# Group norms on ScalarE, and the last image's closing stages in row blocks beside the last scan

## The chip, the cores and the metric

The kernel runs on one core of one Trainium2 chip. The metric is the device time of one execution in microseconds (us), from the first to the last instruction on the core and what lies around it. Before the change the median of three runs is 14916.63 us (14892.47 to 14927.26). Profiles are single executions recorded by the hardware profiler; all times inside the kernel come from such a record.

## The reference

Four images of 96 channels and 64 x 64 points pass through four layers. Every layer is `x = x + layer(gn(x))`, where `gn` is a group norm with 32 groups of 3 channels:

```python
def _gn(v, G=32, eps=1e-5):
    g = v.reshape(B_, G, C_ // G, H_, W_)
    m = jnp.mean(g, axis=(2, 3, 4), keepdims=True)
    s = jnp.var(g, axis=(2, 3, 4), keepdims=True)
    return ((g - m) / jnp.sqrt(s + eps)).reshape(v.shape)
```

Layer 0 is an attention over a sampled image with a neighbourhood step. Layer 1 projects to 192 channels, convolves, and runs a state-space scan of 16 states in four directions (rows forward, rows backward, columns forward, columns backward); the four results are summed, layer-normed, gated and passed through a convolution block. Layer 2 is a 3 x 3 sharpening convolution. Layer 3 has a second such scan, `h = h * exp(d * A) + (d * u) * b`, `y = sum over states of h * c`, again in four directions, followed by what the kernel calls `finish`:

```python
y = oy[:, 0] + inv[:, 0] + why + invwhy            # four directions
y = layernorm(y) * silu(z) @ ow.T                   # norm, gate, output projection
y = x1 + x2 * g                                     # skip branch
y = layernorm over channels
up = conv1x1(y[:48]); low = conv1x1(y[48:])         # squeeze to 24 each
Y1 = conv3x3(up, groups=2) + conv1x1(up); Y2 = concat(conv1x1(low), low)
out = softmax(mean over points of concat(Y1, Y2)) * concat(Y1, Y2)
out = (first half + second half) @ fin_w.T + fin_b
```

Only the mean over all points couples distant rows in this last part; the 3 x 3 convolution couples neighbouring rows; everything else is per point.

## The kernel before

**Scans.** There are eight scans, one per image and scan layer, in the order `SCANS`. A scan has four directions ("ways"), each of 4 chunks of 1024 points and two halves of the channels: 32 groups. A group has 12 units; a unit is 8 channels x 16 states on 128 partitions and 1024 points. So a scan has 384 units, and the kernel 3072. The function `unit` writes one unit's instructions: SyncE fetches `rep` (the step sizes, broadcast) four units ahead (`fetch`, L1827); ScalarE turns it into the decay two units ahead (`decays`, L1835); TensorE spreads the input into PSUM two units ahead (`drive`); VectorE multiplies that by `b` one unit ahead (`times_b`, L1849) and runs the scan (`scan`, L1856); POOL multiplies by `c` (`times_c`, L1868); every third unit TensorE sums the states (`collect`). At the end of a group `output` puts the result into `yo`, and SyncE stores it to `y_row` or `y_col` at the start of the next unit (L1904). The next groups' step sizes and inputs are made by `prepare`, in steps between the units.

**Work beside a scan.** All other layers of the images are Python generators: `first` (layer 0 and the start of layer 1), `second` (the end of layer 1, layer 2, the start of layer 3) and `third` (the end of layer 3). `BESIDE` says which runs beside which scan: scans 0, 3, 4 have a first, scans 1, 2, 5, 6 a second, the last scan the thirds of images 0, 1 and 2. A generator yields a number when it has issued a step; `unit` resumes it up to twice, once ahead of `decays` and once ahead of `times_b`, within a budget: `PACE` (3.5) a unit, less 2.1 in every third unit. What is left of a stage at unit 365 of a scan is written out at once (`work.run()`). The first stage of image 0 runs alone before the scans (to 702 us), the third of image 3 alone after them. Inside the scans the order on each engine is that of the program; each engine works its own instructions in that order.

**Group norm** (L1039): eight `bn_stats` of 512 points and an aggregate on VectorE, two small matmuls that average over the three channels of a group, a root on ScalarE, and four `tensor_scalar` on VectorE that write the result. Each first and each second has two.

**The end of layer 3** (`third`, `finish`). `directions` loads `y_col` and `y_row` and adds them on POOL (L1391). `layer_norm` runs over 8 chunks of 512 points: mean by matmul, subtraction on VectorE (L1153), square on ScalarE (L1155), sum of squares by matmul; then one root (L1165) and one reciprocal (L1167) for all chunks; then per chunk the product and `gate` (L1575, L1576). The output projection adds `skip3` (L1590). A second norm is followed per chunk by `squeeze`; then the convolution, the mean and softmax, and per chunk the final product (L1687), which reads `res2` through tile `o` and stores the result.

Of the kernel before, what the change touches and what calls it, by code (L numbers as in the profile page):

```python
# [9 lines left out]
F32 = mybir.dt.float32  # L10
# [28 lines left out]
          (("first", 3),), (("second", 2),), (("second", 3),), (("third", 0), ("third", 1), ("third", 2)))  # L39
# [854 lines left out]
def streams(ctx: ExitStack, tc: tile.TileContext, x, wts, cst, out, wat, cat, flag):  # L894
# [144 lines left out]
    def group_norm(src, dst):  # L1039

        st = small.tile([96, 8, 6], F32, name="gn_st")
# [23 lines left out]
        for j in range(4):  # L1065
            nc.vector.tensor_scalar(dst[:, 16 * j : 16 * j + 16, :], img(src)[:, 16 * j : 16 * j + 16, :],
                                    g[:, 0:1], g[:, 1:2], ALU.subtract, ALU.mult)
            yield 1
# [67 lines left out]
    def layer_norm(pool, V, n, gains, each):  # L1136

        acc = held()
        sq = {}

        def add(j):
            for h in range(n):
                mm(acc[:8], cv("means")[:96, n - 1, 7 - j : 15 - j], sq.pop((j, h)),
                   j == 0 and h == 0, j == 7 and h == n - 1)

        for j in range(8):
# [5 lines left out]
            for h in range(n):  # L1152
                nc.vector.tensor_sub(V[:, h, js], V[:, h, js], p1[:96])  # L1153
                t = pool.tile([96, PCH], F32, name="ln_sq", bufs=2 * n)
                nc.scalar.activation(t, V[:, h, js], AF.Square)  # L1155
                sq[j, h] = t
            yield n
            if j:
                add(j - 1)
                yield  # L1160
                yield n
        add(7)
        yield
        r = pool.tile([8, PCH], F32, name="ln_r", bufs=1)
        nc.scalar.activation(r, acc[:8], AF.Sqrt, bias=eps[:8])  # L1165
        yield n
        nc.vector.reciprocal(r, r)  # L1167
        yield 3
        for j in range(8):
            js = bass.ts(j, PCH)  # L1170
            p = bank()
            mm(p[:96], ident[:8, j : j + 1].to_broadcast([8, 96]), r)
# [383 lines left out]

    def third(b):

        with tc.tile_pool(name="p3x", bufs=1) as PX:
            V = yield from directions(PX, b)  # L1560
            yield from finish(PX, b, V)

    def finish(PX, b, V):
        with tc.tile_pool(name="p3", bufs=2) as pool:
            w = staged(pool, "l3_in", "l3_out")

            def gate(j):
                js = bass.ts(j, PCH)
                xz = pool.tile([96, PCH], F32, name="xz", bufs=2)
                nc.sync.dma_start(out=xz, in_=gate3[b][:, js])  # L1570
                for h in range(2):
                    p = bank()
                    mm(p[:96], w["l3_in"][:, E + 96 * h : E + 96 * h + 96], xz)
                    yield
                    nc.scalar.activation(p[:96], p[:96], AF.Silu)  # L1575
                    nc.vector.scalar_tensor_tensor(out=V[:, h, js], in0=V[:, h, js],  # L1576
                                                   scalar=wv("l3_ss_outn_b")[:, h : h + 1], in1=p[:96],
                                                   op0=ALU.add, op1=ALU.mult)
                    yield 1

            yield from layer_norm(pool, V, 2, wv("l3_ss_outn_g"), gate)
            for j in range(8):
                js = bass.ts(j, PCH)
                x2 = pool.tile([96, PCH], F32, tag="tmp", name="x2")
                nc.sync.dma_start(out=x2, in_=skip3[b][:, js])
                p = bank()
                for h in range(2):
                    mm(p[:96], w["l3_out"][:, h, :], V[:, h, js], h == 0, h == 1)
                yield
                nc.vector.scalar_tensor_tensor(out=V[:, 0, js], in0=x2, scalar=0.5, in1=p[:96],  # L1590
                                               op0=ALU.mult, op1=ALU.add)
                yield 2
        with tc.tile_pool(name="p4", bufs=2) as pool:

            up = pool.tile([96, PADW, W], F32, name="up", bufs=1)
            for s in (up[:, 0, :], up[:, PADW - 1, :], up[0:32, :, 0:1], up[64:96, :, W - 1 : W]):
                nc.gpsimd.memset(s, 0.0)
            sq3 = pool.tile([96, 3, 32], F32, name="sq3", bufs=1)
            nc.gpsimd.memset(sq3, 0.0)
            gw = pool.tile([96, 3, C], F32, name="gw", bufs=1)  # L1600
            nc.gpsimd.memset(gw, 0.0)
            pw = pool.tile([96, C], F32, name="pw", bufs=1)
# [8 lines left out]
            low = pool.tile([24, L], F32, name="low", bufs=1)  # L1611

            def squeeze(j):
# [13 lines left out]
                mm(q[:24], wv("l3_sq")[:, 1, :], v)  # L1627
                yield
                nc.scalar.copy(low[:, js], q[:24])
                yield 1  # L1630

            yield from layer_norm(pool, V[:, 0:1, :], 1, wv("l3_ln_g"), squeeze)
            w = staged(pool, "l3_y2", "l3_fin")

            sums = pool.tile([96, 2, 8], F32, name="csums", bufs=1)
            for j in range(8):
                js = bass.ts(j, PCH)
                p = bank()
                for t in range(3):
                    mm(p[:96], gw[:, t, :], up[:, 8 * j + t : 8 * j + t + 8, :], t == 0, t == 2)  # L1640
                    if t < 2:
                        yield (1,)
                yield
# [440 lines left out]
```

## Time and profile before

| | us |
|---|---|
| median of 3 runs | 14916.63 |
| profiled execution | 14908.91 |
| its span | 14907.1 |
| image 0's first stage alone | 0 to 702 |
| scans 0 to 6 | 702 to 12661, 1697 to 1719 each |
| scan 7, thirds beside it | 12661 to 14626 |
| image 3's third alone | 14626 to 14907 |

| engine | busy us | share |
|---|---|---|
| PE | 12122.0 | 81% |
| DVE (VectorE) | 11789.6 | 79% |
| POOL | 10381.2 | 70% |
| ACT (ScalarE) | 8282.7 | 56% |

In a group's row of the profile stand the line, the engine, the operation, the tiles written and read with their shapes, the count, the busy time and the mean of one in ns, and then how long the engine stood idle just before such an instruction and what ended that. Matmul ends are modelled, so a busy PE is not a PE at its peak. In answers by windows each row is a stretch of the span with the busy time and count of each engine, the granted TensorE clock, the mean busy share of the DMA engines and their GB/s.

### The profile page before, as it was taken

To read this page: it belongs to the slowest core of one execution; us is meant where nothing else is said; L and a number is where in the kernel's file an instruction comes from. 1 tells how busy PE (TensorE), PEld (TensorE's weight loads), DVE (VectorE), ACT (ScalarE), POOL (GpSimd) and SP (SyncE) were. 2 spreads that over 40 slices of the span, in tenths; PEclk is the share of its full clock that TensorE was granted. 3 is DMA by queue.
4 is the path that set the end of the run, shared out by engine and by line. 5 is a ranking of instruction groups with operands and counts; after the bars stand their busy time and mean duration, and the time that the engine had idled before them with its cause. 6 is when DMAs were issued, how large, how long until landed. Compare 5 with 4: busy or idle time off the path is not lost. (4 is left out here: it accounts for less than half of the span.)

```text
span 14907.1 us, 126739 instructions
## 1 busy us (share of the span) xinstructions
PE 12122.0 (81%) x40354; PEld 3289.6 (22%) x40354; DVE 11789.6 (79%) x7685; ACT 8282.7 (56%) x11648; POOL 10381.2 (70%) x4746
## 2 busy tenths in 40 slices
PE   8788985988879797989878886897969888667757
PEld 2322221222212121222212221222212222111111
DVE  0577888888878888779887898888878888767884
ACT  3255564556745566555655555565745567545652
POOL 0166877877868777668776787787768777656672
PEclk9878886988879787879877897897879888666666
DMA  0266788786878778668876788786878878666682
GB/s 9 66 160 161 193 207 196 188 204 173 218 174 203 186 195 199 171 166 204 210 176 157 178 201 216 176 207 175 205 187 195 199 178 219 169 166 166 166 207 66
DMA packets 902135, 2644.28 MB, mean 177 GB/s; under 512 B 107280, under 2 KB 257392, under 8 KB 901456
## 3 DMA queue, kind: packets, MB, share of 16 engines
q1 hardware_dynamic: 900800, 2634.83, 71.4%
q8 instruction: 320, 5.24, 0.2%
q14 instruction: 359, 2.94, 0.1%
q10 hardware_dynamic: 656, 1.27, 0.0%
HBM read 2169.08 MB, written 466.62 MB: 177 GB/s over the span
## 5 line engine op out<-in xcount | busy, mean ns | idle before, releaser
L1868 POOL TENSOR_TENSOR rep<-hs,bc 128x1024 f32<-128x1024 f32 x3072 | 7236.0, 2360 | 3150.8 <-DVE hs L1856 2691.1
L1856 DVE TENSOR_TENSOR_SCAN hs<-rep,carry,bx 128x1024 f32<-128x1024 f32 x2304 | 5401.0, 2344 | 277.1 <-POOL rep L1868 13.7
L1849 DVE TENSOR_TENSOR bx<-bx,bc 128x1024 f32<-128x1024 f32 x3072 | 3720.0, 1211 | 895.4 <-PE bx L948 860.7
L1835 ACT ACTIVATE rep<-rep,l_decay 128x1024 f32<-128x1024 f32 x3072 | 3495.5, 1143 | 929.3 <-DMA rep<-dd 901.8
L948 PE MATMUL bx<-parts,spread 24*128 24x512 bf16 x6144 | 1412.2, 436 | 1806.4 <-DVE hs L1856 1756.9
L948 PE MATMUL acc<-rep,ct 128*32 128x512 f32 x12288 | 2615.7, 735 | 188.9 <-POOL rep L1868 188.9
L1856 DVE TENSOR_TENSOR_SCAN hs<-rep,bx 128x1024 f32<-128x1024 f32 x768 | 1754.5, 2284 | 312.2 <-POOL rep L1868 229.1
L948 PEld LDWEIGHTS <-spread 24*128 24x128 bf16 x6144 | 310.6, 93 | 4279.2 <-DVE hs L1856 2899.2
L948 PE MATMUL one<-band,dg 96*96 96x512 f32 x2304 | 1119.5, 621 | 0.0
L948 PE MATMUL one<-upad,diag 96*96 96x512 f32 x2016 | 1032.0, 649 | 2.7 <-ACT ur L1128 2.7
L948 PEld LDWEIGHTS acc<-rep,ct 128*32 128x32 f32 x12288 | 508.5, 127 | 1976.2 <-issue 1489.2
L948 PE MATMUL one<-qq,kk 96*128 96x512 f32 x1152 | 818.2, 799 | 135.5 <-ACT ex L1248 81.8
L1248 ACT ACTIVATE ex<-one 128x512 f32<-128x512 f32 x576 | 343.0, 595 | 746.3 <-PE one L948 741.5
L948 PE MATMUL one<-pr,ct 6*96 6x512 f32 x1024 | 648.4, 731 | 36.7 <-ACT pr L1740 4.3
L1835 ACT ACT_TABLE_LOAD x470 | 603.0, 1283 | 112.0 <-DMA rep<-dd 104.1
L948 PE MATMUL one<-hp,diag 96*96 96x512 f32 x1152 | 607.2, 665 | 49.3 <-POOL diag L1075 49.3
L948 PE MATMUL one<-vpad,diag 96*96 96x512 f32 x1200 | 586.5, 624 | 0.0
L1864 ACT COPY carry<-hs 128x1 f32<-128x1 f32 x2304 | 408.5, 177 | 316.3 <-DVE hs L1856 315.3
L948 PE MATMUL held<-ex,cols 128*32 128x256 f32 x3072 | 568.8, 451 | 11.7 <-ACT ex L1248 5.7
L948 PE MATMUL held<-ex,vT 128*32 128x256 f32 x3072 | 569.3, 451 | 0.0
L948 PEld LDWEIGHTS one<-band,dg 96*96 96x96 f32 x2304 | 350.4, 166 | 532.5 <-issue 517.3
L948 PEld LDWEIGHTS one<-upad,diag 96*96 96x96 f32 x2016 | 320.7, 173 | 500.4 <-issue 480.0
(3403 smaller groups left out, 13884.4 us busy)
## 6 DMA issues: line engine op xcount, KB each, us to landing
rep<-dd SPq DMA_DIRECT2D x3072, 512.0 KB
parts<-du SPq DMA_DIRECT2D x1024, 144.0 KB
bc<-rows SPq DMA_DIRECT2D x256, 512.0 KB
dd<-delta SPq DMA_DIRECT2D x256, 384.0 KB
du<-cut SPq DMA_DIRECT2D x256, 384.0 KB
us<-urow SPq DMA_DIRECT2D x128, 384.0 KB
du<-cut SPq DMA_DIRECT2D x256, 192.0 KB
yrow<-yo SPq DMA_DIRECT2D x128, 384.0 KB
```

What stands on the lines that cost most here:

```text
L948: nc.tensor.matmul(o, lhsT=lhsT, rhs=rhs, start=first, stop=last)
L1248: nc.scalar.activation(last.rearrange("p a b -> p (a b)"), p, AF.Exp, scale=HD**-0.5)
L1835: nc.scalar.activation(a, a, AF.Exp, scale=decay[tag][:, k, NG * h + m : NG * h + m + 1])
L1849: nc.vector.tensor_mul(bx, bx, ready[i // NG][2][:, 0, :])
L1856: nc.vector.tensor_tensor_scan(out=hs, data0=a, data1=bx, initial=carry[:, h, m : m + 1] if c else 0.0, op0=ALU.mult, op1=ALU.add)
L1864: nc.scalar.copy(carry[:, h, m : m + 1], live[i][1][:, CH - 1 : CH])
L1868: nc.gpsimd.tensor_tensor(a, hs, ready[i // NG][2][:, 1, :], ALU.mult)
```

## The change

Four things change. A group norm beside a scan is made of ScalarE activations with accumulators; alone, it stays as it was. The third stage of the last image, now `last`, is also beside the last scan: the l3 scans take their column ways first, `last` waits (it yields `WAIT`, which ends the unit's budget) until the column results are stored, turns them into row order with ScalarE copies, and then takes the image in four blocks of two chunks, each as soon as the rows that it needs are stored. `stored` counts stored groups. `finish` takes a list of such blocks; for the other images it is one block of eight chunks. In `finish` the loads of `y_row`, `gate3`, `skip3` and `res2` go through `Ahead`, which starts the next chunk's load when the present one is taken, and the two pools of `finish` are one, with `low` in the partitions 96 to 119 of `up`. `PACE` depends on the stage: 3.5, 3.7 and 3.2. Both versions start a scan's stage at the scan's unit 0. In the last scan nothing is written out at unit 365: what is left runs after the last unit.

```diff
-          (("first", 3),), (("second", 2),), (("second", 3),), (("third", 0), ("third", 1), ("third", 2)))
+          (("first", 3),), (("second", 2),), (("second", 3),), (("third", 0), ("third", 1), ("third", 2), ("last", 3)))
...
     def group_norm(src, dst):
+        if not solo[0]:
+            yield from group_norm_on_scalar(src, dst)
+            return
...
+    def group_norm_on_scalar(src, dst):
+        st = small.tile([96, 8], F32, name="gs_st")
+        for j in range(4):
+            s = src[:, bass.ts(j, CH)]
+            nc.scalar.activation(s, s, AF.Copy, accum_out=st[:, j : j + 1])
+            yield 1
+        mv = small.tile([96, 4], F32, name="gs_mv")
+        nc.vector.tensor_reduce(mv[:, 0:1], st[:, 0:4], AX.X, ALU.add)
+        yield 0.5
+        p = bank()
+        mm(p[:96, 0:1], group[:96], mv[:, 0:1])
+        yield
+        nc.scalar.activation(mv[:, 1:2], p[:96, 0:1], AF.Copy, scale=-1.0 / L)
+        yield 0.5
+        for j in range(8):
+            p = bank()
+            nc.scalar.activation(p[:96], src[:, bass.ts(j, PCH)], AF.Square, bias=mv[:, 1:2], accum_out=st[:, j : j + 1])
+            yield 1
+        nc.vector.tensor_reduce(mv[:, 2:3], st, AX.X, ALU.add)
...
+        nc.scalar.activation(mv[:, 2:3], p[:96, 0:1], AF.Sqrt, bias=eps[:96], scale=1.0 / L)
+        yield 0.5
+        nc.vector.reciprocal(mv[:, 2:3], mv[:, 2:3])
+        nc.vector.tensor_mul(mv[:, 3:4], mv[:, 1:2], mv[:, 2:3])
+        yield 0.5
+        for j in range(4):
+            nc.scalar.activation(dst[:, 16 * j : 16 * j + 16, :], img(src)[:, 16 * j : 16 * j + 16, :], AF.Identity,
+                                 scale=mv[:, 2:3], bias=mv[:, 3:4])
+            yield 1
...
+    class Ahead:
+        def __init__(self, load, chunks):
+            self.load, self.left = load, list(chunks)
+            self.next = load(self.left.pop(0))
+        def get(self):
+            t, self.next = self.next, self.load(self.left.pop(0)) if self.left else None
+            return t
...
+    def last(b):
+        with tc.tile_pool(name="p3x", bufs=1) as PX:
+            V = PX.tile([96, 2, L], F32, name="V", bufs=1)
+            per_way = 2 * NCH
+            first_ = len(groups) - 4 * per_way
+            while stored[0] < first_ + 2 * per_way:
+                yield WAIT
+            with tc.tile_pool(name="turn", bufs=1) as T:
+                for h in range(2):
+                    t = T.tile([96, W, H], F32, name="yc")
+                    for j in range(4):
+                        nc.sync.dma_start(out=t.rearrange("p a b -> p (a b)")[:, bass.ts(j, CH)],
+                                          in_=y_col[h][b][:, bass.ts(j, CH)])
+                    yield 1
+                    for j in range(8):
+                        nc.scalar.copy(img(V[:, h, bass.ts(j, PCH)]),
+                                       t[:, :, 8 * j : 8 * j + 8].rearrange("p a b -> p b a"))
+                        yield 1
+            yield from finish(PX, b, V, [(first_ + 3 * per_way + 2 * k + 2, (7 - 2 * k, 6 - 2 * k)) for k in range(NCH)])
...
     def finish(PX, b, V, blocks):
...
+            todo, there = set(range(8)), {-1, 8}
+            for need, chunks in blocks:
+                while stored[0] < need:
+                    yield WAIT
+                if need:
+                    for h in range(2):
+                        yr = Ahead(loaded("tmp", y_row[h], 3), chunks)
+                        for j in chunks:
+                            v = V[:, h, bass.ts(j, PCH)]
+                            nc.gpsimd.tensor_tensor(v, v, yr.get(), ALU.add)
+                            yield 1
...
+                yield from layer_norm(pool, V, 2, wv("l3_ss_outn_g"), gate, chunks)
...
+                yield from layer_norm(pool, V[:, 0:1, :], 1, wv("l3_ln_g"), squeeze, chunks)
+                there |= set(chunks)
+                for j in sorted(k for k in todo if k - 1 in there and k in there and k + 1 in there):
...
+            o_s = Ahead(loaded("tmp", res2, 3), range(8))
...
-             "l3_": ((0, "r", False), (2, "r", True), (1, "c", False), (3, "c", True))}
+             "l3_": ((1, "c", False), (3, "c", True), (0, "r", False), (2, "r", True))}
...
-    PACE = 3.5
+    PACE = {"first": 3.5, "second": 3.7, "third": 3.2}
...
         while store:
             store.pop()()
+            stored[0] += 1
...
             v = next(self.stage, 0)
+            if v == WAIT:
+                return budget
...
-            if at == per - NG - LEAD - 1:
+            if at == per - NG - LEAD - 1 and s < len(SCANS) - 1:
                 work.run()
-            owed = min(owed, 0.5) + PACE - (2.1 if i % 3 == 1 else 0.0)
+            owed = min(owed, 0.5) + PACE[BESIDE[s][0][0]] - (2.1 if i % 3 == 1 else 0.0)
...
     solo[0] = True
     spare.clear()
-    Slots(third(SCANS[-1][1])).run()
+    work.run()
```

## The prediction

> **What bounds the kernel now.** I read the page first, then the windows of each scan, then windows inside a scan, then groups and waits. The page's busy row and its three costliest kinds give the unit of the kernel:
>
> ```profile
> PE 12122.0 (81%) x40354; PEld 3289.6 (22%) x40354; DVE 11789.6 (79%) x7685; ACT 8282.7 (56%) x11648; POOL 10381.2 (70%) x4746
> ...
> L1856 DVE TENSOR_TENSOR_SCAN hs<-rep,carry,bx 128x1024 f32<-128x1024 f32 x2304 | 5401.0, 2344 | 277.1 <-POOL rep L1868 13.7
> L1849 DVE TENSOR_TENSOR bx<-bx,bc 128x1024 f32<-128x1024 f32 x3072 | 3720.0, 1211 | 895.4 <-PE bx L948 860.7
> L1835 ACT ACTIVATE rep<-rep,l_decay 128x1024 f32<-128x1024 f32 x3072 | 3495.5, 1143 | 929.3 <-DMA rep<-dd 901.8
> ```
>
> A unit is one scan and one product on VectorE: 2.34 + 1.21 = 3.55 us, 3072 times, 10,906 of the 14,907 us. Next, busy time by stretch (us; PE, PEld, DVE, ACT, POOL; then clock, DMA), and the same for the scan line alone, which counts units:
>
> ```profile
> 2417.00:4114.00 1697.00, 1419.38 (x4268) 386.98 (x4268) 1421.90 (x894) 1000.38 (x1360) 1293.18 (x587) 0.84 0.78 193
> 12661.00:14626.00 1965.00, 1321.07 (x3528) 286.81 (x3528) 1546.66 (x1073) 1031.39 (x1474) 1319.98 (x619) 0.68 0.71 175
> ...
> 1933.40:1974.30 40.90, 19.89 (x63) 4.19 (x60) 40.35 (x35) 18.23 (x21) 29.64 (x13) 0.59 0.82 202
> 3216.00:3266.00 50.00, 16.35 (x58) 3.46 (x58) 41.22 (x36) 18.53 (x19) 30.89 (x22) 0.55 0.80 214
> 12661.00:14271.00 1610.00, 1135.14 (x2904) 253.05 (x2904) 1205.77 (x867) 862.27 (x1235) 1018.89 (x487) 0.69 0.68 167
> 14271.00:14626.00 355.00, 185.93 (x624) 33.76 (x624) 340.90 (x207) 169.12 (x240) 301.09 (x132) 0.60 0.88 212
> 14626.00:14907.00 281.00, 219.43 (x338) 51.71 (x338) 67.13 (x96) 66.69 (x120) 25.87 (x26) 0.69 0.11 31
> ...
> 12661.00:14271.00 1610.00, 669.69 (x288) 0.69 0.68 167
> 14271.00:14626.00 355.00, 223.22 (x96) 0.60 0.88 212
> ```
>
> The last scan runs three images' last stages beside its first 288 units, at 1610/288 = 5.59 us a unit, then 96 units alone at 355/96 = 3.70 with VectorE 96% busy, then the fourth image's last stages alone in 281 us. So a bare unit costs about 3.6, and what work adds to that is its **excess**: 1610 - 288 x 3.6 = 573 us for three images, 191 each. VectorE itself is only 75% busy there: most of the excess is waiting in order. In the group-norm window of a "first" stage VectorE is busy 40.35 of 40.9 us; that one is pure VectorE.
>
> **1. Group norms to ScalarE (14 of 16).** These rows price both sides:
>
> ```profile
> L1043 DVE BATCH_NORM_STATS2 gn_st<-xn 96x6 f32<-96x512 f32 x64 | 41.0, 677 | 25.4 <-DMA xn<-in_x 25.3
> L1057 DVE SCALAR_TENSOR_TENSOR gn_v<-gn_d,gn_mv 96x1 f32<-96x1 f32 x16 | 35.4, 2215 | 0.6
> L1066 DVE TENSOR_SCALAR xn<-xn,gn_g 96x1024 f32<-96x1024 f32 x32 | 37.7, 1194 | 0.3
> L1155 ACT ACTIVATE ln_sq<-V 96x512 f32<-96x512 f32 x160 | 98.9, 629 | 313.4 <-DVE V L1153 192.3 <-POOL V L1391 95.1 <-DVE V L1590 17.0
> ```
>
> Removed from VectorE: 8 x 0.68 + 4 x 1.19 + 2.2 + some 0.8 of small ones = 13.2 us; added: two sums, a reciprocal and a product, about 0.8. Added on ScalarE: 4 summing copies and 4 scalings of 1024 columns at 1.14 (nearest row: L1835), 8 squares at 0.63, 12 accumulator reads at 0.19 (the row of L1454): 9.1 + 5.0 + 2.3 = 16.4 us, spread over some 12 units by the budget. Bare, ScalarE has 169/96 = 1.8 us a unit; with 1.4 more it is at 3.2, below 3.55. The Trainium skill, "ScalarE: Activation LUTs", section "Rules for kernel authors", speaks against this: add and multiply belong on VectorE. Taken as the rule, 16.4 replaces 12.4 and 14 norms lose 14 x 4 = 56 us. I take the row: in the window VectorE has no idle time and ScalarE is 18.23 of 40.9 busy. Excess of the norm units now: firsts' second norm 40.9 - 8 x 3.6 = 12 (three), seconds' first 50.0 - 28.8 = 21 (four; 10 of it is VectorE waiting for X to land), seconds' second 44.0 (window 3380 to 3424, 7 units) - 25.2 = 19, say 17 (four), firsts' first 41.0 (5825 to 5866, 7 units) - 25.2 = 16 (three): 238 us. I leave 5 for each of seven and 12 for each of the seven behind a load, because ScalarE then waits for the load ahead of the next decay, which is only two units (7 us) early: 119 stay. **-120**, bounds -200 and +56.
>
> **2. Pace of the seconds, 3.5 to 3.7.** A collection takes 2.1 every third unit, so 2.8 steps a unit become 3.0. In the order of instructions the last activation of a second moves from unit 364 to 345; of a first, whose norms have 9 steps more each, from 339 to 352. Two effects. (a) At 364 the four column stores stand on SP's queue right before the next scan's first load:
>
> ```profile
> 4051.50 3.64 PE L948 MATMUL one<-us,wt 96*38 96x512 f32 x8 [13.70 <-DMA us<-urow]
> ...
> 4058.13 1.23 DVE L1849 TENSOR_TENSOR bx<-bx,bc 128x1024 f32<-128x1024 f32 x1 [13.32 <-PE bx L948]
> ```
>
> With 20 units between them that wait goes, in four scans; the stores still hold SP 3.6 us: 4 x 13.3, **-45** taken. The l3 scans now begin with columns, whose stores come last, but also 20 units before. (b) Denser work leaves more units bare and makes the others longer. PE is busy 1419 of 1697 us; if the busy share stayed as it is, 7% more work a unit would cost up to 38 us a second stage; if it rises into the idle time, nothing. Most units there run at 3.6 and few long ones carry the excess, so I take the low part: 10 each, **+40**, bounds 0 and +150.
>
> **3. The three images beside the last scan.** Pace 3.2 stretches each only from 96 to about 98 units. The loads of res2, skip3 and gate3 move a chunk ahead. Their price now:
>
> ```profile
> L1687 DVE SCALAR_TENSOR_TENSOR o<-one,wt,o 96x512 f32<-96x512 f32 x24 | 17.9, 747 | 88.5 <-DMA o<-res 49.1 <-PE one L948 31.9 <-issue 7.5
> ```
>
> 49 us of VectorE waiting for o, plus 7 for x2 (L1590) and 23 of PE for xz in the waits of 12661 to 14271: **-60**, bounds 0 and -100.
>
> **4. The fourth image.** In the order of instructions its column turn stands at units 292 to 303, row blocks at 314 to 336, 338 to 360 and 362 to 381, the fourth block after the scan. Cost beside: the turn has 4 instead of 8 loads a half and ScalarE copies in place of POOL adds; the present turn has about 41 us of excess in 12 units (7.03 us each), half of it POOL waiting for loads: 20. The blocks: units 12 to 84 of the scan (from the starts of L1856: 5.30, 6.13, 5.23, 5.15, 4.34, 4.71 by twelves) hold the same steps for 8 chunks, excess 111, so 6 chunks 83. Four more reciprocals on VectorE than two norms need, 3.3 each (L1167): 13. The row load waits on SP for the store ahead of it to land, 2.9 us at the tail's L1386 (14642.01), behind it rep fetches two units early: 3 times, and 12 POOL adds: 10. Less 8 of excess already in the bare units: **+118**, bounds +60 and +220. The same page, "Table sets: the hidden batching unit", says to batch activations by set: alone, Silu was loaded once; beside a scan each of 12 Silus and 6 Sqrts needs its set and Exp's again, 36 loads. By the trace's 1.283 us (the row L1575 ACT_TABLE_LOAD) 46 us of ScalarE in 90 units, 0.5 a unit, under VectorE; by the page's 2.66 us with drain, 96 us, 1.1 a unit, still under. I add nothing.
>
> The tail, by windows from 14626.5: scan to last yo 15.5, store and load 10, norm 33, its root and reciprocal 5.6, gates 52, output 16, second norm 19, squeeze 60, convolution 31, softmax 8, final eight chunks 26, end 4: 280. Left after: 15.5, 9.5, 10, 5.6, 13, 4.5, 11, 15, 13 (three chunks), 8, 26, 4 = 135. I take **-140**, bounds -90 and -150.
>
> **The sum** against the profiled span: 14,907 - 120 - 45 + 40 - 60 + 118 - 140 = 14,700. The profiled execution took 2 us more than its span and the median of the runs is 8 above that one: **14,710**.
>
> **Rivals.** (A) ScalarE sets the pace in the norms. For: it waits 901.8 us for rep, so at times its two-unit lead is gone, and every norm step then delays a decay. Against: 44% idle. Decides when a norm's excess exceeds 23 us (8.5 now left plus 207/14); at the full 19 us of ScalarE with table loads and 8 of load wait it is 27: 14,710 + 14 x 18.5 = 14,970, slower. (B) Short blocks beside the scan cost what they save: two-chunk norms leave no other chunk to fill a wait; excess 220 instead of 118, with +40 more from the pace: 14,850. (C) The waits vanish wholly: norms at 3 us, final chunks without waiting, no price of pace: -75, -40, -40: 14,555. (D) Work "from its first unit on" does nothing: work began at unit 0 of each scan before too and the budget starts at 0 in both; it is in no term.
>
> **Chances.** Forecast (14,630 to 14,810) 0.52, C (below) 0.15, B (to 14,887) 0.19, no change 0.04, A 0.10. 0.2% (30 us) is about what a measurement of this kernel can tell from no change. Faster 0.86, same 0.04, slower 0.10. Range 14,590 to 14,875: about one in ten on each side.
>
> **What would show it.** Norm units near 3.9 us, VectorE's busy time down by some 160 us and ScalarE's up by 230 plus the table loads (1); no us wait near the end of scans 1, 2, 5, 6 (2a), their bodies up by no more than 10 us (2b); the wait of o for res2 near zero (3); units 292 to 384 of the last scan at about 4.9 us, tail near 140 (4). I am wrong if ScalarE's waits turn into waits of the scan for the decay, or the blocks' units exceed 6 us.

## The result, and the profile after

The changed kernel takes 14,759.2 us (median of four executions, 14,741.4 to 14,778.6) against 14,908.1 for the kernel before on the same chip: ratio 0.990, 95% interval 0.988 to 0.992. The forecast was 14,710 with a range of 14,590 to 14,875: the right sign, inside the range, and 49 us too low. The profiled execution is the slowest of the four, 14,778.6 us with a span of 14,776.7.

The page of the changed kernel, its busy row and the three groups that make a unit:

```profile
PE 12152.6 (82%) x40354; PEld 3301.0 (22%) x40354; DVE 11667.3 (79%) x7509; ACT 8565.8 (58%) x12123; POOL 10366.0 (70%) x4746
...
L1950 DVE TENSOR_TENSOR_SCAN hs<-rep,carry,bx 128x1024 f32<-128x1024 f32 x2304 | 5401.9, 2345 | 281.4 <-POOL rep L1962 18.0
L1943 DVE TENSOR_TENSOR bx<-bx,bc 128x1024 f32<-128x1024 f32 x3072 | 3723.1, 1212 | 950.7 <-PE bx L948 905.4
L1929 ACT ACTIVATE rep<-rep,l_decay 128x1024 f32<-128x1024 f32 x3072 | 3495.4, 1142 | 645.2 <-DMA rep<-dd 604.4
```

VectorE is busy 122 us less (11,789.6 before), ScalarE 283 more. The span fell by 130, so VectorE's idle time is what it was (3,117 and 3,109 us). The decay waits less for its load (901.8 before, 604.4 now), as ScalarE has more to do in between. The product of a unit waits more for TensorE (860.7 to 905.4).

The prediction's first sign of being wrong was a scan that waits for the decay. What the scan (`hs`) waited for it, before and after (us in total, times), is hardly more, so ScalarE kept its lead:

```profile
  DVE hs L1856: 7.0, 6
```

```profile
  DVE hs L1950: 8.9, 3
```

By windows (us; busy time of PE, PEld, DVE, ACT, POOL; clock, DMA share, GB/s) the second scan, the last scan's first 288 units, its last 96, and the tail:

```profile
2391.50:4087.10 1695.60, 1417.33 (x4268) 386.95 (x4268) 1407.36 (x868) 1035.18 (x1423) 1291.83 (x587) 0.84 0.77 194
12596.60:14156.20 1559.60, 1142.46 (x2878) 249.17 (x2879) 1194.20 (x858) 869.06 (x1238) 1018.29 (x487) 0.68 0.69 170
14156.20:14646.80 490.60, 317.32 (x854) 69.20 (x852) 399.39 (x274) 267.73 (x368) 318.24 (x154) 0.66 0.69 170
14646.80:14776.70 129.90, 90.02 (x142) 22.07 (x136) 31.40 (x42) 24.04 (x42) 6.10 (x4) 0.65 0.12 34
```

Cut at the first unit of each scan, the two profiled executions differ so:

| stretch | before | after | difference | predicted |
|---|---|---|---|---|
| to the first scan | 702 | 692 | -10 | 0 |
| scans 0, 3, 4 (firsts) | 5134 | 5114 | -20 | -33 (norms) |
| scans 1, 2, 5, 6 (seconds) | 6826 | 6790 | -35 | -89 (norms -84, stores -45, dense pace +40) |
| scan 7, units 0 to 288 | 1610 | 1560 | -51 | -60 |
| scan 7, units 288 to 384 | 353 | 491 | +137 | +118 |
| tail | 283 | 130 | -153 | -140 |

The rows add up to -132, where the forecast's make -204. The medians differ by 149, as the profiled execution of the changed kernel is the slowest of the four. The last image and the early loads came out nearly as costed. What is missing is for the most part in the scans with a second. The experiments look there first.

### The profile page after: what moved, and what is told of

Same layout as the page of the kernel before. It is cut to its first block, busy times and chain, and to the rows that moved or that the text cites. A ratio compares the mean times of both kernels' runs of the same rounds, so it can differ in the third digit from the quotient of the medians.

```text
span 14776.7 us, 127045 instructions
## 1 busy us (share of the span) xinstructions
PE 12152.6 (82%) x40354; PEld 3301.0 (22%) x40354; DVE 11667.3 (79%) x7509; ACT 8565.8 (58%) x12123; POOL 10366.0 (70%) x4746
## 4 chain that ended last, share of the span: by engine, by line
PE 49%; DVE 18%; ACT 10%; POOL 7%; DMA 6%; issue 6%; SPq 1%; DVEq 0%; POOLq 0%; ACTq 0%
PE one L948 32%; DVE hs L1950 13%; PE acc L948 9%; PE bx L948 6%; DVE bx L1943 4%; POOL rep L1962 4%; DMA rep<-dd 3%; PE held L948 2%; ACT rep L1929 2%; ACT L1929 1%; DMA yc<-ycol 1%; ACT ex L1287 1%; POOL V L1430 1%; POOL delta L1874 1%; ACT L1871 0%
## 5 line engine op out<-in xcount | busy, mean ns | idle before, releaser
L1943 DVE TENSOR_TENSOR bx<-bx,bc 128x1024 f32<-128x1024 f32 x3072 | 3723.1, 1212 | 950.7 <-PE bx L948 905.4
L1929 ACT ACTIVATE rep<-rep,l_decay 128x1024 f32<-128x1024 f32 x3072 | 3495.4, 1142 | 645.2 <-DMA rep<-dd 604.4
L948 PE MATMUL acc<-rep,ct 128*32 128x512 f32 x12288 | 2646.2, 746 | 162.9 <-POOL rep L1962 162.6
```

The lines of the kernel that those rows point to most:

```text
L948: nc.tensor.matmul(o, lhsT=lhsT, rhs=rhs, start=first, stop=last)
L1929: nc.scalar.activation(a, a, AF.Exp, scale=decay[tag][:, k, NG * h + m : NG * h + m + 1])
L1943: nc.vector.tensor_mul(bx, bx, ready[i // NG][2][:, 0, :])
```

## The experiments

Each kernel was timed against the kernel before on the same chip, but not all on one chip, so two changed kernels are best compared by their ratios. Times are medians. A ratio, with its 95% interval, is made from all executions and need not be the quotient of the two medians. Times of scans come from one profile of each kernel. How far such a figure scatters can be seen where the program is the same: in four profiles of the changed kernel's scans 0 to 6 the firsts took 5111 to 5121 us in all, the seconds 6762 to 6790; with rows first, two profiles differ by 23 in the firsts.

**Norms alone** (the kernel before, with the ScalarE norm):

```diff
     def group_norm(src, dst):
+        if not solo[0]:
+            yield from group_norm_on_scalar(src, dst)
+            return
```

> The kernel before with one part of the change alone: the 14 group norms beside scans are ScalarE activations; pace, order of ways, last image as before. Theory (norms move off the bound engine): the norm units lose 100 to 120 us of excess over 3.55 us a unit, but a second stage is now nine steps longer twice and four of its last activations are left over at unit 364 and written out at once, 5 to 10 us each in four scans: total about 14,830. Rival (ScalarE takes VectorE's place as the bound in the norms, or the nine more steps of each norm only move the excess elsewhere): 14,880 to 14,950.

Measured 14,835.4 against 14,921.3, ratio 0.9953 (0.9939 to 0.9967): some 70 us by the ratio, as the theory had it. The firsts went from 5134 to 5085, the seconds only from 6826 to 6810. The timeline of VectorE in unit 366 of scan 1 shows what stands against the gain in the seconds:

```profile
3985.56 2.35 DVE L1893 TENSOR_TENSOR_SCAN hs<-rep,carry,bx 128x1024 f32<-128x1024 f32 x1
4008.29 1.23 DVE L1886 TENSOR_TENSOR bx<-bx,bc 128x1024 f32<-128x1024 f32 x1 [20.38 <-PE bx L948]
4012.29 2.35 DVE L1893 TENSOR_TENSOR_SCAN hs<-rep,carry,bx 128x1024 f32<-128x1024 f32 x1 [2.77 <-ACT rep L1872]
```

The ScalarE norm has nine steps more. At pace 3.5 the second then isn't finished at unit 365, the rest is written out at once, and the product of the next unit waits 20.4 us behind it. That unit takes 26.7 us instead of 3.6, in each of four scans: 92 us. Not all of this is lost, since the same work would have lengthened other units (see "Pace taken back").

**Pace alone** (the kernel before, seconds at 3.7):

```diff
-    PACE = 3.5
+    PACE = {"first": 3.5, "second": 3.7, "third": 3.5}
...
-            owed = min(owed, 0.5) + PACE - (2.1 if i % 3 == 1 else 0.0)
+            owed = min(owed, 0.5) + PACE[BESIDE[s][0][0]] - (2.1 if i % 3 == 1 else 0.0)
```

> The kernel before with the pace of the second stages 3.7 instead of 3.5 and nothing else. The last activation of a second moves from unit 364 to 335. Theory of the prediction (denser work costs 10 us a second, the wait for the next scan's first load goes, 10 to 13 us each): -10, total about 14,898. Rival (denser work costs 20 to 25 us a second stage, as the sum over the seven scans of the changed kernel suggests): +40, about 14,950. Scans 0, 3, 4 and 7 stay as they were in both.

Measured 14,858.8, ratio 0.9963 (0.9951 to 0.9976): some 55 us faster, more than either account allowed. The seconds fell from 6826 to 6750, 19 each, where the prediction's two terms for the pace make -1. Half of it is the load of `us` at unit 368 (17.4 us on average before, 8.2 here); the rest says that denser work was not dearer on the whole. An exception is the stretch of the band convolution, in windows of scan 1, before and with this pace:

```profile
2659.10:3188.20 529.10, 518.59 (x1659) 154.65 (x1657) 472.88 (x276) 326.69 (x476) 442.44 (x195) 0.97 0.82 199
```

```profile
2635.60:3143.30 507.70, 501.77 (x1614) 151.69 (x1615) 446.33 (x259) 314.68 (x460) 419.28 (x189) 0.99 0.81 197
```

TensorE is busy 98 and 99% there, against 84% over the scan. The stretch holds the same convolutions in 134 and 126 units: eight units less save 21.4 us, 2.7 each, and each costs 3.6 outside. So the band pays 7 us for the pace in this scan, near the 10 that the prediction took for a whole second, and the other stretches gain.

**Norms taken back** (the changed kernel, norms on VectorE):

```diff
     def group_norm(src, dst):
-        if not solo[0]:
-            yield from group_norm_on_scalar(src, dst)
-            return
```

> The changed kernel with the group norms back on VectorE, all else as changed. Theory (each norm on ScalarE is worth 7 to 8 us net of everything): 14,759 + 105 = 14,865. Rival (what the norm windows gain is given back elsewhere in the scans, so that the net is 55): 14,815.

Measured 14,785.5, ratio 0.9917 (0.9887 to 0.9946): 26 us above the changed kernel, not 70, and below both expectations. The firsts took 5180 (5114 with the norms on ScalarE), the seconds 6747 (6790). In the seconds the ScalarE norm seems to cost time at this pace: the changed program took 6762 to 6790 there in four profiles, all above 6747.

**Pace taken back** (the changed kernel, seconds at 3.5):

```diff
-    PACE = {"first": 3.5, "second": 3.7, "third": 3.2}
+    PACE = {"first": 3.5, "second": 3.5, "third": 3.2}
```

> The changed kernel with the pace of the second stages back at 3.5. A second's last four activations are then left over at unit 364 and written out at once. Theory of the prediction (10 us a second for the denser pace; load wait and leftover come back at 15 us a scan): 14,759 - 40 + 60 = 14,780. Rival (the denser pace costs 20 to 25 a second): 14,759 - 90 + 60 = 14,730, faster than the changed kernel.

Measured 14,772.5, ratio 0.9903 (0.988 to 0.9925): 13 us above the changed kernel, inside the intervals. The unit of 26.7 us is back in all four scans, but the other units are shorter by nearly as much: the seconds took 6799. The total is near the theory's 14,780, but not by its terms: neither the leftover nor the thinner pace shows in the sum.

**The last image alone again** (the changed kernel without `last` beside the last scan):

```diff
-          (("first", 3),), (("second", 2),), (("second", 3),), (("third", 0), ("third", 1), ("third", 2), ("last", 3)))
+          (("first", 3),), (("second", 2),), (("second", 3),), (("third", 0), ("third", 1), ("third", 2)))
...
-    work.run()
+    Slots(third(SCANS[-1][1])).run()
```

> The changed kernel, but the last image's third stage runs alone after the scans again, in one block of eight chunks; norms, pace, order of ways, loads ahead as changed. Reading of the two traces: the first 288 units of the last scan (three thirds) lost 51 us, its last 96 units gained 137, the part after the scans lost 153, so blocks beside the scan are worth only 16: expected 14,775, last scan about 1,910 us, tail 270 to 280. Rival (the blocks disturb the thirds too, or the loads ahead shorten the tail by themselves): 14,740 or less. Theory of the prediction: 14,759 + 22.

Measured 14,783.4 against 14,917.4, ratio 0.9906 (0.987 to 0.9941). The tail of this kernel by its window:

```profile
14508.00:14797.00 289.00, 222.25 (x340) 52.39 (x340) 68.36 (x96) 66.71 (x120) 28.58 (x28) 0.68 0.12 33
```

289 us alone, against 130 in the changed kernel; the last 96 units are 367 here and 491 there. So the blocks bring 159 and cost 124: 35 us net in these two stretches and 20 over the whole span, as the stretches ahead of them happened to take 15 less here. By the medians it is 24, near the forecast's 22, with intervals that overlap. A bare unit is no free place: VectorE was 96% busy in these 96 before the change.

**Thirds at 3.5** (the changed kernel, 3.5 beside the last scan):

```diff
-    PACE = {"first": 3.5, "second": 3.7, "third": 3.2}
+    PACE = {"first": 3.5, "second": 3.7, "third": 3.5}
```

> The changed kernel with the pace beside the last scan 3.5 instead of 3.2. If the 51 us that the three thirds lost come from the loads that are issued a chunk ahead, they stay: within 10 us of 14,759. If they come from the thinner pace, about 45 us of it goes: 14,800.

Measured 14,734.8, ratio 0.9873 (0.9844 to 0.9902): below the changed kernel, which no account had foreseen, though the two intervals overlap. Its windows of the last scan:

```profile
12573.80:14127.10 1553.30, 1118.08 (x2904) 251.41 (x2904) 1204.53 (x865) 860.40 (x1231) 1017.96 (x487) 0.71 0.70 172
14127.10:14600.10 473.00, 316.11 (x830) 64.90 (x830) 395.66 (x266) 275.01 (x375) 317.96 (x155) 0.64 0.70 171
```

The first 288 units cost the same (1560 at 3.2, and 1533 to 1553 in six other profiles at 3.2), the last 96 are 18 us shorter; in five other profiles with the blocks at 3.2 they took 490 to 494, so this difference is no scatter. All of it is in units 288 to 312, the first windows here, of the changed kernel and of this one; the blocks behind them take the same:

```profile
14156.20:14282.00 125.80, 67.17 (x188) 14.15 (x186) 89.01 (x59) 58.70 (x84) 79.04 (x44) 0.59 0.81 208
14282.00:14646.80 364.80, 250.16 (x666) 55.05 (x666) 310.38 (x216) 209.03 (x286) 239.20 (x111) 0.68 0.64 157
```

```profile
14127.10:14234.00 106.90, 53.19 (x160) 9.61 (x160) 84.32 (x51) 65.01 (x90) 79.01 (x45) 0.55 0.91 220
14234.00:14600.10 366.10, 262.92 (x670) 55.28 (x670) 311.35 (x216) 210.00 (x286) 238.96 (x111) 0.67 0.63 156
```

The row of the final product in the changed kernel (shortest, median and longest ns; first and last start) tells why:

```profile
L1780 DVE SCALAR_TENSOR_TENSOR tmp<-one,wt,tmp x24: 721/747/747, 13087.8 to 14184.8; 96x512 f32<-96x512 f32 x24
```

The third image's last product starts at 14,184.8, 29 us behind the start of unit 288 (14,156.2). At 3.2 three images do not fit into 288 units, and their end stands in units 288 to 291; at 3.5 it is through in unit 287.

**Squares twice** (the changed kernel, each of the norms' squares issued twice; the values are the same):

```diff
             nc.scalar.activation(p[:96], src[:, bass.ts(j, PCH)], AF.Square, bias=mv[:, 1:2], accum_out=st[:, j : j + 1])
+            nc.scalar.activation(p[:96], src[:, bass.ts(j, PCH)], AF.Square, bias=mv[:, 1:2], accum_out=st[:, j : j + 1])
```

> The changed kernel with each of the eight squares of a group norm on ScalarE issued twice (the second overwrites the first with the same values), 8 x 0.87 = 7 us more of ScalarE for each of 14 norms, no step more for the budget. If ScalarE has room there: within 20 us of 14,759. If ScalarE sets the pace of the norm units: + 7 x 14 = +98, 14,857.

Measured 14,780.3, ratio 0.9901 (0.9873 to 0.9929), as the changed kernel's 0.990 (the medians, from two chips, differ by 21). 112 more squares with their accumulator reads are 97 us of ScalarE. About a quarter of it shows, as the stretches of the 14 norms (cut at the scans around them) took 23 us more; all 97 would lie outside the two intervals. ScalarE does not set the pace in the norms, and rival A falls.

**Columns first alone** (the kernel before, only the order of the l3 ways changed):

```diff
-             "l3_": ((0, "r", False), (2, "r", True), (1, "c", False), (3, "c", True))}
+             "l3_": ((1, "c", False), (3, "c", True), (0, "r", False), (2, "r", True))}
```

> The kernel before with only the order of the ways of layer 3's scans changed: columns first, then rows. Theory of the prediction (costs nothing where second stages end early): here a second ends at unit 364 and its column stores come right before the next scan's first load, now of columns: that load also waits for the stores to land, + 3 to 5 us in two scans, about 14,915. Rival (the row ways' products on VectorE, now in units 192 to 383, cost about 20 us beside the convolution of the first stage in scan 3): 14,930 to 14,940, with scan 3 alone 20 us longer.

Measured 14,927.6, ratio 1.0003 (0.9991 to 1.0016): free in sum. By scans it is not nothing. Scan 3, with a first beside it, is 33 us longer (the rival had 20), and scan 2, with a second, 27 shorter. Over all profiles scan 3 took 1715 to 1740 us with columns first and 1684 to 1707 with rows first. The firsts took 5191 (5134 before), the seconds 6772 (6826); but in this pair scans 0, 1, 4 and 5, whose order did not change, moved by up to 21, so these sums are rough.

**Rows first** (the changed kernel, columns first in the last scan alone):

```diff
-              for k, axis, back in KINDS[tag] for c in range(NCH) for h in range(2)]
+              for k, axis, back in (KINDS[tag] if s == len(SCANS) - 1 else sorted(KINDS[tag], key=lambda w: w[1] == "c"))
+              for c in range(NCH) for h in range(2)]
```

> The changed kernel, but only the last scan takes its columns first; scans 2, 3 and 6 keep rows first as before the change. The question is why norms (-70 alone) and pace (-55 alone) are worth only some 56 us together in scans 0 to 6 (11,960 us before; 11,895 with norms alone and with pace alone; 11,905 in the changed kernel). Theory 1, the order of the ways takes it: with columns first scans 0 to 6 took 11,928 (pace) and 11,926 (norms), 31 us more each than with rows first; then scans 0 to 6 fall by some 30 to 70 us, to 11,835 to 11,875, and the time to about 14,710 (14,690 to 14,730). Theory 2, norms and dense pace take it from each other (the norm's 9 extra steps move the rest of a second back among other units): scans 0 to 6 stay at 11,885 to 11,910 and the time at 14,745 to 14,765.

Measured 14,734.7, ratio 0.9878 (0.9863 to 0.9894). Scans 0 to 6 took 11,908 us, as in the changed kernel (11,905): theory 1 falls by its own number, and norms and pace take it from each other with rows first too. The time is lower than the 14,745 that theory 2 allowed, but the trace shows that the order is not the cause: this profile's span is 26 us below the changed kernel's, and units 0 to 288 of the last scan, where the two programs are the same, took 1533 instead of 1560.

The scans of all these executions in one table (us; the last row is the changed kernel and the three runs that share its scans 0 to 6; the second figure with rows first is the last run below):

| norms on ScalarE | pace of seconds | l3 ways | firsts | seconds |
|---|---|---|---|---|
| no | 3.5 | rows | 5134 | 6826 |
| yes | 3.5 | rows | 5085 | 6810 |
| no | 3.7 | rows | 5145 | 6750 |
| yes | 3.7 | rows | 5092, 5069 | 6815, 6819 |
| no | 3.5 | columns | 5191 | 6772 |
| yes | 3.5 | columns | 5127 | 6799 |
| no | 3.7 | columns | 5180 | 6747 |
| yes | 3.7 | columns | 5112 to 5121 | 6762 to 6790 |

In the firsts the norms are worth 49 to 76 us in every pair. In the seconds they are worth 16 with pace 3.5 and rows first, and cost 15 to 69 in the other pairs; only the 65 and 69, with pace 3.7 and rows first, are well outside the scatter. The sums over the four seconds, pace alone and then with the norms (rows first), show where:

```profile
sum 6750.20, PE 5595.65 PEld 1538.44 DVE 5714.82 ACT 3987.66 POOL 5174.94; mean PE 1398.91 PEld 384.61 DVE 1428.71 ACT 996.91 POOL 1293.74
```

```profile
sum 6815.40, PE 5673.94 PEld 1550.73 DVE 5646.20 ACT 4117.78 POOL 5168.07; mean PE 1418.48 PEld 387.68 DVE 1411.55 ACT 1029.45 POOL 1292.02
```

VectorE does 69 us less, as meant; TensorE is busy 78 us more with the same number of matmuls, and the scans take 65 us more. Cut by the lines that begin and end a part, the loss is in the convolutions of the output block and in the input projection behind the norms, not in the norms: the former took 268.8 us for 59 units (mean of four scans) with the pace alone, and 284.5 for 60 with both. In scan 1 the windows of it, pace alone and both:

```profile
3402.40:3673.10 270.70, 246.03 (x711) 69.70 (x712) 211.50 (x127) 177.21 (x231) 193.86 (x85) 0.87 0.73 180
```

```profile
3402.40:3687.10 284.70, 256.01 (x718) 71.93 (x718) 214.43 (x129) 182.02 (x227) 199.02 (x88) 0.85 0.66 172
```

The same steps meet other units there, as the norms ahead of them have more steps. The clock is 0.85 instead of 0.87, but whether that or the matmuls' modelled ends or another order against the collections makes TensorE's time longer is not settled by these runs.

**Thirds at 3.8** (as thirds at 3.5, with 3.8):

```diff
-    PACE = {"first": 3.5, "second": 3.7, "third": 3.2}
+    PACE = {"first": 3.5, "second": 3.7, "third": 3.8}
```

> The changed kernel with pace 3.8 instead of 3.2 beside the last scan; 3.5 gave 14,735 against 14,759. Theory 1, the gain at 3.5 came from the blocks of the last image ending earlier in their 24 units (units 288 to 384 fell from 491 to 473 us with the tail unchanged): then 3.8 gives some 10 to 15 us more, 14,715 to 14,730, with units 288 to 384 near 460. Theory 2, the gain was that the three images end before unit 288, which 3.5 already does: then 3.8 gives nothing more, 14,730 to 14,745. Theory 3, denser steps collide on VectorE (the reason to choose 3.2): first 288 units longer by 20 or more, 14,755 or above.

Measured 14,815.3, ratio 0.9928 (0.9913 to 0.9944): theory 3. The windows of the last scan:

```profile
12575.90:14201.90 1626.00, 1137.53 (x2904) 249.36 (x2904) 1203.14 (x866) 883.32 (x1253) 1019.04 (x497) 0.68 0.66 167
14201.90:14684.00 482.10, 299.40 (x831) 63.21 (x832) 393.56 (x267) 255.38 (x357) 317.17 (x145) 0.67 0.64 159
```

The first 288 units are 73 us longer than at 3.5, and VectorE is no busier. The three images are through at unit 252 and the last image's turn at 263 (its row below, with first and last start), but the rows for its first block are stored only at unit 312: units 264 to 312 run at 3.6 to 3.8 us, and the same work is packed into fewer units ahead of them.

```profile
L1629 ACT COPY V<-yc x16: 1041/1070/1110, 14073.3 to 14110.3; 96x512 f32<-96x512 f32 x16
```

VectorE's waits in the first 288 units, at 3.8 and then at 3.5 (us in total, times, longest):

```profile
DVE V L1709 <- ACT one L1708: 68.3, 39, 3.8
DVE V L1192 <- PE one L948: 54.8, 30, 5.8
DVE V L1214 <- PE one L948: 35.2, 21, 4.9
```

```profile
DVE V L1709 <- ACT one L1708: 46.9, 34, 3.6
DVE V L1192 <- PE one L948: 35.0, 23, 3.9
DVE V L1214 <- PE one L948: 22.8, 23, 2.7
```

Three lines of gate and layer norm wait 54 of the 73 us more. VectorE works in program order, so the scan stands behind the waiting instruction. That the operand from ScalarE or TensorE is now issued too shortly ahead fits this, but no run separates it from other reasons.

**Seconds at 4.0:**

```diff
-    PACE = {"first": 3.5, "second": 3.7, "third": 3.2}
+    PACE = {"first": 3.5, "second": 4.0, "third": 3.2}
```

> The changed kernel with pace 4.0 instead of 3.7 in the second stages. By the prediction's own step (denser work lengthens its units, 10 us a second stage for 0.2 of pace) 0.3 more costs 15 each: 14,820. By the other reading of the run with the pace alone (the body of a second costs no more when denser, because idle time of VectorE fills) nothing is lost, and nothing is gained either, as the last stores already leave 20 units before the next scan's first load: 14,745 to 14,770.

Measured 14,942.7, ratio 1.0021 (1.0014 to 1.0028): slower than the kernel before. Above the changed kernel it is 184 us, three times the 60 that the prediction's rate gives, and far from the other reading. The seconds took 6966 instead of 6790. The band of scan 1, its window and what the product waits for in it:

```profile
2602.80:3089.80 487.00, 482.25 (x1520) 147.93 (x1517) 402.68 (x233) 289.15 (x423) 376.77 (x171) 0.99 0.73 181
```

```profile
DVE bx L1943 <- PE bx L948: 53.6, 62, 4.6
```

From 126 to 113 units it saves 20.7 us, 1.6 a unit, near TensorE's own work for a bare unit (185.93/96 = 1.94, shown in the prediction). Each unit driven out costs 3.6 elsewhere: 26 us net in this scan, and about 104 of the 176 if the other three are like it. Where the rest arose was not followed up. The Trainium skill ("Trainium Kernel Development and Optimization", "Performance Expectations") warns that busy time of matmuls is a bad metric for how near a kernel is to its roofline, as they are pipelined; so the bound rests here not on the 99% but on the time per unit, which falls to TensorE's share once the stretch is full.

**Both that gained** (rows first, and 3.5 beside the last scan):

```diff
-    PACE = {"first": 3.5, "second": 3.7, "third": 3.2}
+    PACE = {"first": 3.5, "second": 3.7, "third": 3.5}
...
-              for k, axis, back in KINDS[tag] for c in range(NCH) for h in range(2)]
+              for k, axis, back in (KINDS[tag] if s == len(SCANS) - 1 else sorted(KINDS[tag], key=lambda w: w[1] == "c"))
+              for c in range(NCH) for h in range(2)]
```

> Rows first in scans 2, 3 and 6 (14,735 with it against 14,759) and pace 3.5 beside the last scan (14,735 against 14,759) together. If both differences are real and independent, 14,710 (14,700 to 14,722). If the first was the scatter of the medians, as its unchanged scans 0 to 6 (11,908 against 11,905 us) say, only the blocks' 18 us in units 288 to 384 stay: 14,730 to 14,745, with those units near 473.

Measured 14,723.2 (14,719.1 to 14,724.2), ratio 0.9871 (0.9854 to 0.9887): the fastest kernel here, each of its executions below each of the changed kernel's. Units 288 to 384 took 470 us. It lies between the two expectations. The pace of the thirds is in it for certain; the order of the ways is not to be seen, as scans 0 to 6 took 11,888 us, against 11,885 in the run with the thirds at 3.5 alone.

## Why the prediction was right, and where it was off

**1. Norms, -120.** The rows of the changed kernel (shortest, median and longest ns, first and last start):

```profile
L1078 ACT ACTIVATE X<-X x32: 1037/1046/1057, 3155.7 to 11825.0; 96x1024 f32<-96x1024 f32 x32
L1090 ACT ACTIVATE one<-X,gs_mv x64: 667/682/687, 3169.2 to 11846.4; 96x512 f32<-96x512 f32 x64
L1090 ACT ACTIVATION_READ_ACCUMULATOR one<-X,gs_mv x64: 185/186/188, 3169.8 to 11847.0; 96x1 f32 x64
L1103 ACT ACTIVATE X<-X,gs_mv x16: 1228/1236/1242, 3352.5 to 11863.9; 96x1024 f32<-96x1024 f32 x16
```

4 x 1.05 + 4 x 1.23 + 8 x 0.68 + 12 x 0.19 = 16.8 us against the 16.4 taken. The mechanism holds, and ScalarE has room for it (squares twice). Alone, the norms gave 70; within the norm stretches of the four seconds, cut at the lines that begin and end them, the excess over 3.55 us a unit fell by 63, where 84 was taken; those of the firsts fell by some 40, where 33 was taken (cut at the scans around them; 58 to 73 for the seconds by such cuts). So the term itself, -120, is nearly right. That the firsts show only -20 in the first table is due to something for which the prediction had no term: columns first lengthens scan 3 by some 30 us ("Columns first alone"). (The forecast's list of excesses also adds up to 236, not 238.)

VectorE's busy time fell by 161 with the norms alone, where 14 x 12.4 = 174 was taken, and by 122 in the changed kernel, where 160 was taken. Part of what is missing is one product of 96 x 1 in each norm, 11.0 and 22.4 us for the 14 (see the last section).

The rule that speaks for VectorE, cited in the prediction, was rightly set aside in the firsts; in the seconds at the dense pace the time is on its side, but by what comes behind the norms, not by what an activation costs.

**2. Pace, -45 and +40.** The wait for `us` at the end of scan 1 shrank, but stayed; TensorE, and the product behind it:

```profile
4023.72 3.79 PE L948 MATMUL one<-us,wt 96*38 96x512 f32 x8 [4.92 <-DMA us<-ucol]
...
4030.83 1.23 DVE L1943 TENSOR_TENSOR bx<-bx,bc 128x1024 f32<-128x1024 f32 x1 [5.48 <-PE bx L948]
```

Unit 368 took 17.4 us on average and takes 8.9 now: -34 instead of -45. The stores ahead of the load are gone, the wait for the load itself is not. What is left of the seconds' -35 when this and the norm stretches' -63 are taken off is +62, where +40 was taken.

So the step that failed is the sum of steps 1 and 2. Each was costed as if the other were not made. Measured in scans 0 to 6 from 11,960 us on, the norms alone give 65, the pace alone 65, and both with rows first 52 and 72 (two profiles), where the sum of the two would be 130. What in the second order makes TensorE's time longer stays open. For the pace alone the sign of the body was wrong too: its +40 is found in the band (+5 to 12 a scan), but other stretches took the denser work into idle time. The mean TensorE share of 84% hid the band's 98%.

**3. Loads ahead, -60.** Measured: -51. The final product still waits, but the load is a small part (us, times):

```profile
L1780 DVE SCALAR_TENSOR_TENSOR tmp<-one,wt,tmp x24: 721/747/747, 13087.8 to 14184.8; 96x512 f32<-96x512 f32 x24
...
  PE one L948: 24.2, 13
  DMA tmp<-res: 10.2, 5
```

10 us for the load instead of 49. The pace can be kept apart: with the thirds at 3.5, as before the change, the three images end in unit 287, as before, and the 288 units took 1553 and 1550 us (two kernels) against 1610 to 1621 in four kernels without the early loads: -57 to -71, as forecast. The early loads came with more buffers and one pool instead of two, and no run separates these. The stretching by pace 3.2 was noted (98 units an image, the turn from unit 292 on), but given no price; it cost 18 us in units 288 to 312.

**4. The last image, +118 and -140.** Measured: +137 and -153; the difference is -16 where -22 was forecast. Of the 137, 13 are the end of the third image, which stands behind unit 288 also where the last image runs alone; the blocks cost 124, against 118. The dearer price of a table load that the prediction weighed does not show: the loads took 1.283 us, and in the median the next activation started 0.01 us after a load. The block units are 5.1 us, under the 6 that would have spoken for B. B, that blocks cost what they save, is nearly true all the same, since the forecast itself had the gain at 22 only.

The rivals: A is refuted, C too (the `us` wait and VectorE's waits for gate and norm operands remain), and D says nothing that could be measured, as both versions start at unit 0. The 10 us ahead of the first scan were in no step: the ten profiles with ScalarE norms enter it at 689 to 698 us, the four with VectorE norms at 700 to 703. The norm beside scan 0 no longer lets VectorE wait for its input ahead of the first scan, as here in the kernel before:

```profile
700.45 1.28 DVE L1043 BATCH_NORM_STATS2 gn_st<-xn 96x6 f32<-96x512 f32 x2 [13.33 <-DMA xn<-in_x]
701.65 2.27 DVE L1856 TENSOR_TENSOR_SCAN hs<-rep,bx 128x1024 f32<-128x1024 f32 x1
```

## What to carry to other kernels

Two edits that move the same interleaved work are not additive: cost the second in the order that the first leaves behind, and try each one alone and both together. A pace has an optimum that is found stretch by stretch: look for the stretch in which another engine is full (here TensorE at 98% in the band, 84% in the mean), since denser work there drives out units that cost their full price elsewhere. Before work is moved beside a loop, ask whether the loop's bare units have the engine's time to hide it; here 159 us taken from the tail cost 124 beside the scan.

One combination was not tried: ScalarE norms in the firsts alone, VectorE norms in the seconds, with rows first and 3.5 beside the last scan. By the table the seconds would be 69 us below those of the fastest kernel (6750 against 6819), which puts it near 14,655. That is an estimate, and it adds two edits, which this case warns of.

## What was not expected of the hardware

TensorE's busy time in the four seconds rose by 78 us (5595.65 to 5673.94) at the same 17,072 matmuls, when only ScalarE's and VectorE's instructions ahead had changed. The mean clock is 0.83 to 0.85 in each of the eight scans. And the response to the pace is steep: in the thirds 3.2, 3.5 and 3.8 gave 14,759, 14,735 and 14,815; in the seconds 3.5, 3.7 and 4.0 gave 14,773, 14,759 and 14,943.

A third thing was found in the norms. Their last small product, of 96 x 1, took 155 ns at the shortest and 3361 at the longest (a mean of 1602 in the changed kernel, 22.4 us for 14). One of the longest with the two POOL products of that time, and one of the shortest with its neighbour on POOL:

```profile
3186.43 3.36 DVE L1100 TENSOR_TENSOR gs_mv<-gs_mv 96x1 f32<-96x1 f32 x1
3185.12 4.65 POOL L1962 TENSOR_TENSOR rep<-hs,bc 128x1024 f32<-128x1024 f32 x2
```

```profile
1988.11 0.16 DVE L1100 TENSOR_TENSOR gs_mv<-gs_mv 96x1 f32<-96x1 f32 x1
1988.19 2.36 POOL L1962 TENSOR_TENSOR rep<-hs,bc 128x1024 f32<-128x1024 f32 x1 [0.74 <-DVE gs_mv L1099]
```

All nine that took over 1.3 us began while such a POOL product ran and ended within 0.02 us of one's end; the five of 0.16 us began with POOL idle. The norm before shows the same: its row L1057 took 2215 ns in the mean, but 0.21 and 0.22 us in the two norms ahead of the scans. So the price of a small instruction was in part a wait for POOL that the trace counts as busy time; no run here was made to test it.
